# A two-layer kernel with a mixture of experts: queue places by products, logits read in PSUM, turned inputs written by ScalarE, four result buffers

## The chip, the cores and the metric

One core of a Trainium2 chip runs the whole program. The time is the device time of that core in microseconds (us), from the first to the last instruction of one execution; less is better. The kernel before takes 1167.64 us, the median of three runs (1167.55 to 1169.25).

## The reference, cut to what matters

Two layers run one after the other on `x`, 4 batches of 512 tokens of 256 values, all in float32. Layer 0 is the one that the change touches:

```python
h = _layernorm(x) * (1 + ca) + sa               # ca, sa, ga ...: per batch, from silu(c) @ wmod
q, k, v = split(h @ W + b, 3)
x = x + ga * (q / |q| * sum_t(k / |k| * v))     # norms and sum over the 512 tokens
h = _layernorm(x) * (1 + cb) + sb
...
logits = h @ gate_w.T                           # 2048 tokens x 32 experts, in 8 groups of 4
# the 3 groups with the largest maximum are kept, the other logits become 0; softmax;
# the 6 largest are chosen, weights times 16
pos = cumsum(one_hot(chosen)) - 1               # place in the expert's queue, token after token
valid = pos < 48                                # an expert takes 48 tokens, the rest get zero
act = silu(xb @ w_gate) * (xb @ w_up)           # per expert, inner size 176
yb = act @ w_down
out = sum_k(topk_w * yb[slot]) + shared_experts(h)
x = x + gb * out
```

Layer 1 is causal attention with 16 heads of 128 for each batch and a gated feed-forward net whose weights are interpolated from control points.

## The kernel before, in words

Tokens lie on the 128 partitions: a batch is four tiles of 128 tokens (`NTT` = 4). A product needs the values on the partitions instead, so every norm ends in transpositions on TensorE (PE) and an eviction that also applies the modulation. The program runs in three stages.

**The front** (0 to 150.3 us) goes through the batches. `attention_input` normalises a batch and turns it; `linear_attention`, in two halves, projects v, k and q and forms the attention; `attention_output` turns the result back and adds it to x; `moe_input` is the second norm, turned into `hTs[b]`; `choose` makes logits and picks six experts for each token; `table_rows` writes the tokens to a table in DRAM, its arithmetic on GpSimd (POOL, L534 and L535); `place` finds each token's place in its expert's queue. Each engine works off its instructions in order. In the front that order is made by the framework's scheduler from the program, which puts the products of the shared experts (`shared`, L704), which need only `hTs`, between the others on PE. After the last batch a small product (`pid`, L686) gives the list of tokens for every expert.

What the change touches there:

- `ln_transposed` (L217): for each half k of the 256 values, four transpositions (L226) into a PSUM tile of tag "tr", and one eviction: k = 0 by ScalarE (ACT, L228), k = 1 by VectorE (DVE, L232). The tag has two banks, shared in the front with the attention's output on its way back (`add_transposed`, L237) and with the logits.
- `choose` (L542): eight products put the logits into a bank of tag "tr" (L547); DVE copies them to SBUF (L555), reduces them to group maxima (L559), finds the three best (`max`, L562, `match_replace`, L566), makes the mask `keep` (L568) and multiplies (L572); softmax is a maximum (L580), a subtraction, ACT's exp (L584), a sum and a division. L592 to L595 turn probabilities into keys (a probability below `TINY` gets a low key), L598 to L604 choose six, `selb` being the 0/1 matrix in bf16. L608 and L610 then form `pre`: for each tile of 128 tokens, the number of choices that lie in earlier tiles and earlier batches, kept for each partition and each expert; `carry` hands it from batch to batch.
- `place` (L615): two products make the place. `tri` (L619), 1 where the row of the token is below, counts the choices in the same tile; `ones` (L622) sums `pre` over the partitions. L626 then adds -200 where the token is chosen, L628 adds 200 and cuts at 255, so that tokens not chosen end at a large number: `posb`. Its one-hot form against 48 places (L650) goes through products with the token numbers (L654) into `ixs` (L661). The tiles `pos`, `pix` and `pid` share one bank, tag "lgix".

**The experts** (150.3 to 237.3 us) are 16 pairs of experts, 64 rows each. The order on PE is written out by hand here: gather (`xg`), transposition, `gate_up` (L805), `act_turned`, `down` (L828), with the shared experts' second product between them. Weights have 8 slots, loaded by SP's queue. `down` leaves a pair's result in PSUM (`y`, one bank), and ACT writes it, times the token's weight, to an SBUF tile `ysb` (L842). For pairs 0 to 11 that tile has tag "ysb", of two buffers, and two DMAs read it: POOL's scatter to `planes` (L858), for the tokens of batch 0, and SP's write to `ytab` (L873), from which the other batches gather later. Pairs 12 to 15 have tag "ysd", four buffers, and come to batch 0 through a product instead of a scatter. Then SP reads `planes` back (L912) and DVE sums.

**Layer 1** (from 248 to 1166 us) begins with the norm of batch 0. It calls `ln_transposed` too.

Of the kernel before, what the change touches and what calls it, by code (L numbers as in the profile page):

```python
# [10 lines left out]
F32 = mybir.dt.float32  # L11
BF16 = mybir.dt.bfloat16
I32 = mybir.dt.int32
AF = mybir.ActivationFunctionType
ALU = mybir.AluOpType
AX = mybir.AxisListType

P = 128
B, T, D = 4, 512, 256
NT = B * T  # L20
NTT = T // P
# [4 lines left out]
E, G, TOPG, TOPK, CAP, INT = 32, 8, 3, 6, 48, 176  # L26
# [7 lines left out]
NDIR = 4  # L34
NEARLY = 6
TINY = float(np.finfo(np.float32).tiny)
# [44 lines left out]
def kernel(ctx: ExitStack, tc: tile.TileContext, a: dict, out: bass.AP):  # L81
    nc = tc.nc
# [19 lines left out]
    SA, CA, GA, SB, CB, GB = range(6)  # L102
# [111 lines left out]
                )  # L214
        return xn

    def ln_transposed(pool, psum, tag, layer, b, shift, scale, hT, name, bufs=None, after=None, scalar_after=None):  # L217

        xn = normalized(pool, b, name, bufs, after, scalar_after)
        for k in range(2):  # L220
            if isinstance(tag, tuple):
                pt = psum.tile([P, T], F32, tag=tag[k], name=f"lt_{name}{b}{k}", bufs=1)
            else:
                pt = psum.tile([P, T], F32, tag=tag, name=f"lt_{name}{b}{k}")
            for i in range(NTT):
                nc.tensor.transpose(pt[:, i * P : (i + 1) * P], xn[:, i, k * P : (k + 1) * P], ident)  # L226
            if k == 0:
                nc.scalar.activation(  # L228
                    hT[:, k, :], pt, AF.Identity, bias=mv(layer, shift, k, b), scale=mv(layer, scale, k, b)
                )  # L230
            else:
                last = nc.vector.tensor_scalar(  # L232
                    hT[:, k, :], pt, mv(layer, scale, k, b), mv(layer, shift, k, b), ALU.mult, ALU.add
                )
        return xn, last
# [66 lines left out]
    with ExitStack() as l0:  # L302
        moe = l0.enter_context(tc.tile_pool(name="moe", bufs=1))
        front = ExitStack()
        fc = front.enter_context(tc.tile_pool(name="frontc", bufs=1, side="right"))
        rp = front.enter_context(tc.tile_pool(name="route", bufs=2, side="right"))
# [15 lines left out]
        )  # L322
        didx = moe.tile([P, NPAIR], I32, tag="didx", name="didx")

        carry = fc.tile([P, E], BF16, tag="carry", name="carry")
        nc.gpsimd.memset(carry, 0.0)

        zeroed, last, hTa = [], {}, {}
        with tc.tile_pool(name="mod0", bufs=1) as mp:
# [13 lines left out]
            with tc.manual_schedule(engines={mybir.EngineType.PE}):  # L343
# [19 lines left out]
                out=wsd[:, 0:2, :], in_=a["ws_down"][0 : 2 * P].rearrange("(c p) n -> p c n", p=P)  # L363
            )
            nc.sync.dma_start(out=wsd[0 : SHC[2], 2, :], in_=a["ws_down"][2 * P : 2 * INT])
            for v, src in enumerate((S0[64:68, D:], S0[96:100, 0:D], g4)):
# [3 lines left out]
                out=rows.rearrange("p v b d -> p (v b d)"),  # L370
                in_=flat[:, 0 : 2 * B * D].to_broadcast([P, 2 * B * D]),
            )
            nc.sync.dma_start(
                out=gbr.rearrange("p b d -> p (b d)"),
                in_=flat[:, 2 * B * D :].to_broadcast([P, B * D]),
# [8 lines left out]
            for i in range(NTT):  # L384
                fill = nc.sync.dma_start(
                    out=planes[i * P * TOPK : (i + 1) * P * TOPK, :].rearrange("(p r) d -> p (r d)", p=P),
                    in_=zero,
                )
# [3 lines left out]
        def constants():  # L392

            tri = fc.tile([P, P], BF16, tag="tri", name="tri")
            nc.gpsimd.memset(tri, 1.0)
            nc.gpsimd.affine_select(
                out=tri, in_=tri, compare_op=ALU.is_gt, fill=0.0, base=0,
                pattern=[[1, P]], channel_multiplier=-1,
            )
            ones = fc.tile([P, P], BF16, tag="ones", name="ones")  # L400
            nc.gpsimd.memset(ones, 1.0)
            iota_c = fc.tile([P, CAP, E], BF16, tag="iota_c", name="iota_c")
            nc.gpsimd.iota(
                iota_c, [[1, CAP], [0, E]], base=0, channel_multiplier=0,
                allow_small_or_imprecise_dtypes=True,
            )

            tok = fc.tile([P, NI, 32], BF16, tag="tok", name="tok")
            nc.gpsimd.memset(tok, 0.0)
            nc.gpsimd.iota(  # L410
                tok[:, :, 0], [[0, NI]], base=0, channel_multiplier=1, allow_small_or_imprecise_dtypes=True
            )
            nc.gpsimd.iota(
                tok[:, :, 1], [[P, NI]], base=-NT, channel_multiplier=0, allow_small_or_imprecise_dtypes=True
            )

            two = fc.tile([P, 4], F32, tag="two", name="two")
            nc.gpsimd.memset(two, 0.0)
            for q in range(4):
                nc.gpsimd.memset(two[32 * q : 32 * q + 2, q : q + 1], 1.0)  # L420

            six = fc.tile([P, NTT, 1], F32, tag="six", name="six")
            nc.gpsimd.iota(
                six, [[P * TOPK, NTT], [0, 1]], base=0, channel_multiplier=TOPK,
                allow_small_or_imprecise_dtypes=True,
            )

            first = moe.tile([P, 1, E], F32, tag="first", name="first")
            nc.gpsimd.iota(
                first, [[0, 1], [EPAD, E]], base=1, channel_multiplier=0,  # L430
                allow_small_or_imprecise_dtypes=True,
            )

            gss, dps = [], []
            for u in range(2):
                gs = fc.tile([P, NTT, 16], F32, tag=f"gs{u}", name=f"gs{u}")
                nc.gpsimd.memset(gs[:, :, G:], 3.0e38)
                gss.append(gs)
                dp = fc.tile([P, NTT, E + 8], F32, tag=f"dp{u}", name=f"dp{u}")
                nc.gpsimd.memset(dp[:, :, E:], 1.0)  # L440
                dps.append(dp)

            ixs = fc.tile([P, EPAD, 8], F32, tag="ixs", name="ixs")
            nc.gpsimd.memset(ixs, 0.0)

            return tri, ones, iota_c, tok, two, six, first, gss, dps, ixs
# [28 lines left out]
        hTs, posbs = {}, {}  # L475

        def attention_input(b, sp, ps):
            hT = hTa[b] = sp.tile([P, 2, T], F32, tag="hTa", name=f"hT_a0{b}")
            _, last[b] = ln_transposed(sp, ps, "tr", 0, b, SA, CA, hT, "a0", 3, last[b - 1])

        oTs0, xns = {}, {}

# [41 lines left out]
        def moe_input(b, sp, ps):  # L524

            hTs[b] = new_hT(hp, b, "m0")
            xn, _ = ln_transposed(sp, ps, "tr", 0, b, SB, CB, hTs[b], "m0", 3)
            xns[b] = xn

        def table_rows(b):  # L530
# [9 lines left out]
        chosen = {}  # L540

        def choose(b, ps):  # L542

            lgv = ps.tile([P, NTT, E], F32, tag="tr", name=f"plg{b}")
            for i in range(NTT):
                for k in range(2):
# [4 lines left out]
                        start=(k == 0),  # L551
                        stop=(k == 1),
                    )
            lg = rp.tile([P, NTT, E], F32, tag="lg", name=f"lg{b}")
            nc.vector.tensor_copy(lg, lgv)  # L555
            lg4 = lg.rearrange("p i (g j) -> p i g j", g=G)

            gs, dp = gss[b % 2], dps[b % 2]
# [24 lines left out]
            wt = wr[:, :, 0, :]  # L583
# [5 lines left out]


            sel = rp.tile([P, NTT, E], F32, tag="sel", name=f"sel{b}")
            nc.vector.tensor_single_scalar(sel, wt, TINY, ALU.is_ge)  # L592
            nc.vector.tensor_tensor(sc, sc, sel, ALU.mult)
            nc.vector.tensor_scalar(sel, sel, -1.0, 100.0, ALU.add, ALU.mult)
            nc.vector.tensor_tensor(dp[:, :, 0:E], sc, sel, ALU.add)  # L595
            m8 = rp.tile([P, NTT, 8], F32, tag="m8", name=f"em8{b}")
            for i in range(NTT):
                nc.vector.max(m8[:, i, :], dp[:, i, 0:E])  # L598
# [4 lines left out]
            selb = rp.tile([P, NTT, E], BF16, tag="selb", name=f"selb{b}")  # L603
            nc.vector.tensor_single_scalar(selb, dr[:, :, 0:E], 1.5, ALU.is_gt)  # L604
            nc.vector.scalar_tensor_tensor(wt, wt, SCALE, selb, ALU.mult, ALU.mult)

            pre = rp.tile([P, NTT, E], BF16, tag="pre", name=f"pre{b}")
            nc.vector.tensor_copy(pre[:, 0, :], carry)  # L608
            for i in range(NTT):
                nc.vector.tensor_tensor(  # L610
                    pre[:, i + 1, :] if i + 1 < NTT else carry, pre[:, i, :], selb[:, i, :], ALU.add
                )
            chosen[b] = sel, selb, pre, wr

        def place(b):  # L615

            sel, selb, pre, wr = chosen[b]
            pos = psa.tile([P, NTT, E], F32, tag="lgix", name=f"pos{b}", bufs=1)
            nc.tensor.matmul(  # L619
                pos.rearrange("p i e -> p (i e)"), lhsT=tri, rhs=selb.rearrange("p i e -> p (i e)"), start=True, stop=False  # L620
            )
            nc.tensor.matmul(  # L622
                pos.rearrange("p i e -> p (i e)"), lhsT=ones, rhs=pre.rearrange("p i e -> p (i e)"), start=False, stop=True
            )

            nc.vector.scalar_tensor_tensor(sel, selb, -200.0, pos, ALU.mult, ALU.add)  # L626
            posb = posbs[b] = moe.tile([P, NTT, E], BF16, tag=f"posb{b}", name=f"posb{b}")
            nc.vector.tensor_scalar(posb, sel, 200.0, 255.0, ALU.add, ALU.min)  # L628
            if b:

                nc.gpsimd.memset(wr[:, :, 1, :], float(1 << 20))
# [147 lines left out]
        with tc.tile_pool(name="eps", bufs=2, space=PSUM) as ps:  # L779
# [43 lines left out]
            def down(q):  # L823
                wd = loaded[q][1]
                py = ps.tile([P, D], F32, tag="y", name=f"y{q}", bufs=1)
                for c in range(2):
# [7 lines left out]
                        )  # L834
                direct = q >= NPAIR - NDIR
                ysb = xp.tile(
                    [P, D], F32, tag=("ysb", "ysd")[direct], name=f"ysb{q}", bufs=(2, NDIR)[direct]
                )
                for j in range(2):
                    rows_ = slice(EPAD * j, EPAD * j + EPAD)  # L840
# [966 lines left out]
```

## Time and profile before

| What | Value |
|---|---|
| median of three runs | 1167.64 us (1167.55 to 1169.25) |
| the profiled execution's own time | 1168.07 us |
| its span, from first to last recorded work | 1166.0 us |
| mean granted PE clock | 0.993 |
| PE busy (share of the span) | 1118.2 us (96%), 5220 products |
| PE weight loads | 821.9 us (70%) |
| DVE | 859.4 us (74%), 2601 instructions |
| ACT | 536.2 us (46%), 1373 |
| POOL | 619.4 us (53%), 944 |
| DMA | 86.09 MB, mean 74 GB/s |

How to read it: the profile is one execution, recorded by the chip. "Busy" adds up the durations of an engine's instructions; a share of 96% over the whole span says little of a single stage, so the tables of the prediction are cut by stage. In a group of instructions, "out<-in" gives the program's names of the tiles, "L610" the line, "x12" how often, and then stand the busy time, the mean duration in ns and the idle time of the engine just before, with what ended it. "PEclk" or "granted clock" is the share of full speed that TensorE was given. The span is cut in 40 slices on the page, of 29 us each; these are the rows of PE and DVE in tenths of busy time, 9 being 90% or more:

```profile
PE   6888998989999999999999999999999999999998
DVE  5688624567878887788877887988877777567765
```

The first five or six slices are the front, the next three the experts, and the rest layer 1.

### The profile page before, as it was taken

The page shows a single profiled execution, that of the slowest core. Times are in us where ns is not written, and L with a number is a line of the kernel's source. Part 1 is how long each engine was busy: PE and PEld are TensorE (multiplying, and loading weights), DVE is VectorE, ACT ScalarE, POOL GpSimd, SP SyncE. Part 2 cuts the span into 40 slices and gives each one's busy share as a digit, 9 for nine tenths or more (in the row PEclk, how much of TensorE's full clock was granted, in tenths as well). Part 3 has the DMA queues.
Part 4 walks back from the last instruction along what each step waited for, and adds up shares of the span by engine and source line. Part 5 has one row for each costly group of instructions (what it writes and reads, how often), then busy time and mean ns, then how long its engine had stood idle before and what let it go on. Part 6 is the DMA issues. An engine that isn't in the chain of part 4 may idle for free.

```text
span 1166.0 us, 16905 instructions
## 1 busy us (share of the span) xinstructions
PE 1118.2 (96%) x5220; PEld 821.9 (70%) x5220; DVE 859.4 (74%) x2601; ACT 536.2 (46%) x1373; POOL 619.4 (53%) x944
## 2 busy tenths in 40 slices
PE   6888998989999999999999999999999999999998
PEld 2434354557777787777777777777777777888887
DVE  5688624567878887788877887988877777567765
ACT  3543223335555555554555465555555455333321
POOL 3354124338874857864665975444635655344331
PEclk9998999999999999999999999999999999999999
DMA  8910389734411322420321431012010000000001
GB/s 266 292 61 23 101 238 281 237 106 87 85 47 51 73 69 37 86 73 19 86 37 46 95 64 60 28 37 65 23 46 19 22 16 1 1 1 19 19 1 37
DMA packets 80485, 86.09 MB, mean 74 GB/s; under 512 B 12158, under 2 KB 64748, under 8 KB 80268
## 3 DMA queue, kind: packets, MB, share of 16 engines
q1 hardware_dynamic: 67868, 70.19, 19.2%
q0 software_dynamic: 11712, 13.25, 7.1%
q10 hardware_dynamic: 816, 1.58, 0.4%
q8 instruction: 42, 0.69, 0.3%
q14 instruction: 47, 0.39, 0.1%
HBM read 73.84 MB, written 11.55 MB: 73 GB/s over the span
## 4 chain that ended last, share of the span: by engine, by line
PE 64%; DVE 8%; POOL 3%; ACT 2%; issue 1%; DMA 1%; SPq 0%; ACTq 0%; DVEq 0%; POOLq 0%
PE s L1299 10%; PE o L1340 10%; PE po L1035 7%; PE P0p L1035 6%; PE fP L1035 6%; PE pt L1331 5%; PE P1p L1035 4%; PE P2p L1035 4%; PE acc L1035 3%; PE P0v L1035 3%; PE P2v L1035 2%; PE P1v L1035 2%; DMA w_q<-in_w_q 1%; POOL ysum L281 1%; DVE spw L1130 1%
## 5 line engine op out<-in xcount | busy, mean ns | idle before, releaser
L1314 ACT ACTIVATE p<-s,nm 128x512 f32<-128x512 f32 (+3 forms) x256 | 135.2, 528 | 116.0 <-DVE nm L1311 113.9
L1299 PE MATMUL s<-qk,qk 128*128 128x512 f32 (+3 forms) x512 | 170.1, 434 | 1.4 <-DVE qk L1207 1.3
L1340 PE MATMUL o<-pT,v 128*128 128x512 f32 (+3 forms) x512 | 148.6, 433 | 0.1
L1340 PEld LDWEIGHTS o<-pT,v 128*128 128x128 f32 x512 | 96.8, 190 | 55.0 <-issue 30.6
L1333 ACT COPY pT<-pt 128x512 f32<-128x512 f32 (+1 forms) x192 | 98.3, 512 | 67.8 <-PE pt L1331 66.7
L1311 DVE TENSOR_REDUCE nm<-s 128x1 f32<-128x512 f32 (+3 forms) x256 | 124.0, 485 | 4.0
L281 POOL DMA_INDIRECT ysum<-ytab,code x72 | 113.5, 1576 | 20.4 <-issue 15.2
L1316 DVE TENSOR_SCALAR p<-p,den 128x512 f32<-128x512 f32 (+3 forms) x256 | 116.2, 454 | 3.4
L1331 PEld LDWEIGHTS pt<-ident,p 128*128 128x128 f32 x640 | 81.6, 141 | 34.4 <-issue 10.5
L1331 PE MATMUL pt<-ident,p 128*128 128x128 f32 x640 | 101.7, 273 | 0.4 <-DVE p L1316 0.4
L1309 DVE TENSOR_TENSOR s<-s,mask 128x128 f32<-128x128 f32 x256 | 73.4, 287 | 32.6 <-PE s L1299 32.6
L1174 POOL TENSOR_TENSOR w_p<-w_q,w_k 128x128 f32<-128x128 f32 x63 | 38.6, 613 | 85.2 <-ACT t1p L1213 52.3
L1299 PEld LDWEIGHTS s<-qk,qk 128*128 128x128 f32 x512 | 77.5, 191 | 5.8 <-issue 1.4
L1035 PE MATMUL P0p<-hT_a,w_q 128*128 128x256 f32 x252 | 75.0, 379 | 0.0
L1182 POOL TENSOR_TENSOR w_p<-w_k 128x128 f32<-128x128 f32 x63 | 29.7, 472 | 81.4 <-PE P2p L1035 81.4
L1035 PEld LDWEIGHTS P0p<-hT_a,w_q 128*128 128x128 f32 x252 | 47.5, 190 | 33.1 <-issue 29.9
L1315 DVE RECIPROCAL den<-den 128x1 f32<-128x1 f32 x256 | 40.4, 158 | 38.3 <-ACT p L1314 33.6
L1035 PE MATMUL P1p<-fT,w_p 128*128 128x256 f32 x252 | 64.9, 380 | 2.4 <-POOL w_p L1176 1.3
L1351 ACT ACTIVATE oH<-o,bia 128x512 f32<-128x512 f32 x64 | 43.9, 687 | 42.9 <-PE o L1340 41.7
L1207 DVE SCALAR_TENSOR_TENSOR qk<-P0p,bia,u3p 128x256 f32<-128x256 f32 x63 | 30.4, 482 | 37.4 <-ACT qk L1228 36.4
L1043 POOL TENSOR_TENSOR fI<-it 128x256 f32<-128x256 f32 x30 | 21.8, 726 | 67.1 <-DVE it L1632 67.1
L1035 PEld LDWEIGHTS P1p<-fT,w_p 128*128 128x128 f32 x252 | 47.6, 190 | 9.9 <-issue 1.8
(338 smaller groups left out, 2677.7 us busy)
## 6 DMA issues: line engine op xcount, KB each, us to landing
wg<-in_w_gate_up SPq DMA_DIRECT2D x16, 704.0 KB
w_q<-in_w_q SPq DMA_DIRECT2D x64, 128.0 KB
w_k<-in_w_k SPq DMA_DIRECT2D x64, 128.0 KB
w_v<-in_w_v SPq DMA_DIRECT2D x16, 512.0 KB
wd<-in_w_down SPq DMA_DIRECT2D x16, 352.0 KB
basis<-in_basis SPq DMA_DIRECT2D x8, 640.0 KB
planes<-zero SPq DMA_DIRECT2D x4, 768.0 KB
yr<-planes SPq DMA_DIRECT2D x4, 768.0 KB
```

The source lines that it names most:

```text
L281: ga = nc.gpsimd.indirect_dma_start(out=ysum[b][:, i, :], out_offset=None, in_=ytab[:, :], in_offset=bass.IndirectOffsetOnAxis(ap=code[:, ...
L1035: nc.tensor.matmul(out, lhsT=lhsT, rhs=rhs, start=start, stop=stop, skip_group_check=shared)
L1299: nc.tensor.matmul(s[:, at[i] : c], lhsT=qk[n, 0][:, i * P : (i + 1) * P], rhs=qk[n, 1][:, : (i + 1) * P], start=True, stop=True,)
L1309: nc.vector.tensor_tensor(s[:, e - P : e], s[:, e - P : e], mask, ALU.add)
L1311: nc.vector.tensor_reduce(nm, s[:, e - w : e], AX.X, ALU.max, negate=True)
L1314: nc.scalar.activation(p, s[:, e - w : e], AF.Exp, bias=nm, accum_out=den)
L1315: nc.vector.reciprocal(den, den)
L1316: nc.vector.tensor_scalar_mul(p, p, den)
L1331: nc.tensor.transpose(pt[:, c : c + P], probs[n, i][:, j * P : (j + 1) * P], ident)
L1333: nc.scalar.copy(pT, pt[:, :w])
L1340: nc.tensor.matmul(o[:, j * P :], lhsT=vs[n // 4][:, j, hc : hc + HD], rhs=pTs[n, j], start=(j == 0), stop=(j == NTT - 1),)
L1351: nc.scalar.activation(oT, o, AF.Identity, bias=bia[:, 2, h : h + 1])
```

## The change

1. `ln_transposed` gets an argument `both`. Where it is set, in `attention_input` and `moe_input` of layer 0 (three and four calls), ACT does both evictions. Layer 1 is as before.
2. The logits are not copied: L559 and L572 read them in PSUM, so their bank is held until the product with `keep`.
3. L592 to L595, four DVE instructions, become three.
4. `tri` gets -200 on its diagonal, through one more GpSimd mask instruction. The -200 of L626 thereby comes out of the product, and L626 goes; `posb` is made from PSUM directly.
5. The running sums in `pre` go. For each batch but the last, DVE adds up its four `selb` tiles and the carry before (3, 4 and 4 additions). The place is made by products alone: `tri` with `selb`, `ones` with the carry (repeated for all four tiles), and `ones` with each earlier tile (repeated for the later ones): 4 products for batch 0 and 5 for each other batch, 19 in place of 8.
6. Tag "ysb" has four buffers instead of two.

The core of the diff:

```diff
-            if k == 0:
-                nc.scalar.activation(
+            if k == 0 or both:
+                last = nc.scalar.activation(
...
+            nc.gpsimd.affine_select(
+                out=tri, in_=tri, compare_op=ALU.not_equal, fill=-200.0, base=0,
+                pattern=[[1, P]], channel_multiplier=-1,
+            )
...
-            _, last[b] = ln_transposed(sp, ps, "tr", 0, b, SA, CA, hT, "a0", 3, last[b - 1])
+            _, last[b] = ln_transposed(sp, ps, "tr", 0, b, SA, CA, hT, "a0", 3, last[b - 1], both=True)
...
-            xn, _ = ln_transposed(sp, ps, "tr", 0, b, SB, CB, hTs[b], "m0", 3)
+            xn, _ = ln_transposed(sp, ps, "tr", 0, b, SB, CB, hTs[b], "m0", 3, both=True)
...
-            lg = rp.tile([P, NTT, E], F32, tag="lg", name=f"lg{b}")
-            nc.vector.tensor_copy(lg, lgv)
+            lg = lgv
...
-            nc.vector.tensor_single_scalar(sel, wt, TINY, ALU.is_ge)
-            nc.vector.tensor_tensor(sc, sc, sel, ALU.mult)
-            nc.vector.tensor_scalar(sel, sel, -1.0, 100.0, ALU.add, ALU.mult)
-            nc.vector.tensor_tensor(dp[:, :, 0:E], sc, sel, ALU.add)
+            nc.vector.scalar_tensor_tensor(sc, wt, TINY, sc, ALU.is_ge, ALU.mult)
+            nc.vector.tensor_scalar(sel, wt, TINY, -1.0, ALU.is_ge, ALU.add)
+            nc.vector.scalar_tensor_tensor(dp[:, :, 0:E], sel, 100.0, sc, ALU.mult, ALU.add)
...
-            pre = rp.tile([P, NTT, E], BF16, tag="pre", name=f"pre{b}")
-            nc.vector.tensor_copy(pre[:, 0, :], carry)
-            for i in range(NTT):
-                nc.vector.tensor_tensor(
-                    pre[:, i + 1, :] if i + 1 < NTT else carry, pre[:, i, :], selb[:, i, :], ALU.add
-                )
-            chosen[b] = sel, selb, pre, wr
+            chosen[b] = selb, wr
+            if b + 1 < B:
+
+                c = carry[b + 1] = rp.tile([P, 1, E], BF16, tag="carry", name=f"carry{b}")
+                parts = [selb[:, i, :] for i in range(NTT)] + ([carry[b][:, 0, :]] if b else [])
+                nc.vector.tensor_tensor(c[:, 0, :], parts[0], parts[1], ALU.add)
+                for x in parts[2:]:
+                    nc.vector.tensor_tensor(c[:, 0, :], c[:, 0, :], x, ALU.add)
...
+            nc.tensor.matmul(pos, lhsT=tri, rhs=selb, start=True, stop=False)
+            if b:
+                nc.tensor.matmul(
+                    pos, lhsT=ones, rhs=carry[b].to_broadcast([P, NTT, E]), start=False, stop=False
                 )
...
+            for i in range(1, NTT):
+                nc.tensor.matmul(
+                    pos[:, i:, :],
+                    lhsT=ones,
+                    rhs=selb[:, i - 1 : i, :].to_broadcast([P, NTT - i, E]),
+                    start=False,
+                    stop=(i == NTT - 1),
+                )
...
-            nc.vector.scalar_tensor_tensor(sel, selb, -200.0, pos, ALU.mult, ALU.add)
             posb = posbs[b] = moe.tile([P, NTT, E], BF16, tag=f"posb{b}", name=f"posb{b}")
-            nc.vector.tensor_scalar(posb, sel, 200.0, 255.0, ALU.add, ALU.min)
+            nc.vector.tensor_scalar(posb, pos, 200.0, 255.0, ALU.add, ALU.min)
...
-                    [P, D], F32, tag=("ysb", "ysd")[direct], name=f"ysb{q}", bufs=(2, NDIR)[direct]
+                    [P, D], F32, tag=("ysb", "ysd")[direct], name=f"ysb{q}", bufs=4
```

More of the change, by code (lines that the diff above doesn't have):

```diff
@@ L215, in normalized, with ln_transposed @@
         return xn
-    def ln_transposed(pool, psum, tag, layer, b, shift, scale, hT, name, bufs=None, after=None, scalar_after=None):
+    def ln_transposed(pool, psum, tag, layer, b, shift, scale, hT, name, bufs=None, after=None, scalar_after=None, both=False):
         xn = normalized(pool, b, name, bufs, after, scalar_after)
@@ L323 @@
         didx = moe.tile([P, NPAIR], I32, tag="didx", name="didx")
-        carry = fc.tile([P, E], BF16, tag="carry", name="carry")
-        nc.gpsimd.memset(carry, 0.0)
+        carry = {}
         zeroed, last, hTa = [], {}, {}
@@ L605, in choose @@
             nc.vector.scalar_tensor_tensor(wt, wt, SCALE, selb, ALU.mult, ALU.mult)
-            pre = rp.tile([P, NTT, E], BF16, tag="pre", name=f"pre{b}")
-            nc.vector.tensor_copy(pre[:, 0, :], carry)
-            for i in range(NTT):
-                nc.vector.tensor_tensor(
-                    pre[:, i + 1, :] if i + 1 < NTT else carry, pre[:, i, :], selb[:, i, :], ALU.add
-                )
-            chosen[b] = sel, selb, pre, wr
[L615 to L620, printed above, removed]
-            )
[L622 to L626, printed above, removed]
+            chosen[b] = selb, wr
@@ new lines, in choose, with place @@
+            if b + 1 < B:
[4 more added lines that the diff above has]
+                    nc.vector.tensor_tensor(c[:, 0, :], c[:, 0, :], x, ALU.add)
+        def place(b):
+            selb, wr = chosen[b]
+            pos = psa.tile([P, NTT, E], F32, tag="lgix", name=f"pos{b}", bufs=1)
+            nc.tensor.matmul(pos, lhsT=tri, rhs=selb, start=True, stop=False)
+            if b:
+                nc.tensor.matmul(
+                    pos, lhsT=ones, rhs=carry[b].to_broadcast([P, NTT, E]), start=False, stop=False
+                )
+            for i in range(1, NTT):
[6 more added lines that the diff above has]
+                )
```

## The prediction

> **What bounds the kernel now.** First, the busy time of each engine by stage: stretch and length in us, then PE, weight load, DVE, ACT and POOL in busy us (instructions), granted PE clock, DMA share, GB/s.
>
> ```profile
> 0.00:60.00 60.00, 46.36 (x158) 21.63 (x159) 36.66 (x131) 25.75 (x50) 23.06 (x54) 0.97 0.85 278
> 60.00:130.00 70.00, 58.73 (x231) 27.25 (x231) 61.50 (x248) 26.36 (x45) 28.30 (x44) 0.95 0.19 61
> 130.00:150.30 20.30, 20.30 (x75) 8.30 (x74) 8.23 (x14) 2.98 (x5) 7.90 (x8) 1.00 0.24 63
> 150.30:237.30 87.00, 82.51 (x461) 46.78 (x459) 41.45 (x145) 29.20 (x70) 27.35 (x30) 0.98 0.85 262
> 237.30:248.00 10.70, 7.30 (x21) 4.06 (x22) 5.61 (x13) 3.18 (x6) 5.55 (x9) 0.84 0.22 78
> 248.00:1166.00 918.00, 903.05 (x4281) 713.89 (x4279) 705.93 (x2053) 448.73 (x1199) 527.20 (x799) 1.00 0.19 44
> ```
>
> From 248 us on (layer 1) PE is busy 98% of the time, and the built programs have the same order there on every engine; what is won or lost earlier is passed on whole. All edits lie in the front (to 150.3) and the experts (150.3 to 237.3). In the front's middle, 60 to 130 us, DVE is the fullest engine (61.5 of 70 us); PE idles 70 - 58.7 = 11.3 us and runs at clock 0.95 (3.5 us lost). From 130 us PE has no gap: it works off the shared expert's products, which wait for little. So the front ends when PE's fixed work plus its gaps are over; the gaps can be won.
>
> Second, who PE waits for from 10 to 150 us (total us, times, longest), then the groups of instructions up to 150 us that the edits touch (busy us, mean ns | idle before).
>
> ```profile
> PE lt_a L226 <- DVE xn_a L212: 6.4, 5, 2.1
> PE pix L654 <- DVE oh L650: 3.0, 5, 0.9
> PE su L704 <- DVE sT L713: 2.7, 2, 1.6
> PE lt_m L226 <- DVE xn_m L212: 2.5, 4, 1.0
> ```
>
> ```profile
> L610 DVE TENSOR_TENSOR pre<-pre,selb 128x32 bf16<-128x32 bf16 x12 | 4.5, 377 | 0.1
> L232 DVE TENSOR_SCALAR hT_m<-lt_m,mod 128x512 f32<-128x512 f32 x4 | 3.2, 803 | 0.0
> ...
> L626 DVE SCALAR_TENSOR_TENSOR sel<-selb,pos 128x128 f32<-128x128 bf16 x4 | 1.1, 281 | 0.1
> ```
>
> ```profile
> L228 ACT ACTIVATE hT_m<-lt_m,mod 128x512 f32<-128x512 f32 x4 | 3.1, 769 | 0.8 <-PE lt_m L226 0.8
> ```
>
> PE's waits name DVE; ACT is busy for 26 of the 70 us. Third, the experts: who waits (115 to 290 us), and PE in order of time (start, us, what, idle before it).
>
> ```profile
> PE y L828 <- ACT ysb L842: 4.2, 4, 1.9
> ...
> ACT ysb L842 <- DMA ytab<-ysb: 8.2, 3, 3.7
> ...
> ACT ysb L842 <- DMA planes<-ysb,didx: 4.6, 2, 3.3
> ```
>
> ```profile
> 177.55 1.08 PE L828 MATMUL y<-wd,actT 88*64 88x256 f32 x8 [1.02 <-ACT ysb L842]
> ...
> 189.87 1.75 PE L828 MATMUL y<-wd,actT 88*64 88x256 f32 x8 [1.92 <-ACT ysb L842]
> 191.40 2.43 PE L805 MATMUL gu<-wg,xT 128*64 128x352 f32 x8
> ...
> 240.50 0.41 PE L226 MATMUL lt_a<-ident,xn_a 128*128 128x128 f32 x2 [3.24 <-DMA basis<-in_basis]
> ```
>
> All four PE waits from pair 2 to the last scattered pair end at a ysb write on ACT, and ACT waits there for DMAs that still read the buffer of two pairs before: about 10 us from issue (the table write of pair 0 is issued at 166.19; ACT goes on at 176.55), while a pair takes 3 to 4 us. The last wait (240.50; the DMA named there feeds no transposition) ends a chain: last scatter issued at 214.7, planes read back from 217.3, DVE sums from 225.3 to 234.8, norm, transposition. It starts from pair 11, so it moves with it.
>
> **The change, part by part.** Sums are against the profiled execution (1168.07 us, span 1166.0); the median of the runs is 0.4 lower.
>
> *DVE in the front.* Removed: seven turned inputs, 7 x 0.80 = 5.6 us; four logit copies (L555, 0.286 each) 1.1; four rounds of L592 to L595 (0.341 + 0.392 + 0.216 + 0.409 = 1.36 each) become three instructions priced like L593, L592 and L595 (1.14): 0.9; L608 and L610 (4 x 0.168 + 12 x 0.377 + 4 x 0.284 = 6.3) become 11 additions (3, 4, 4, none): at 0.377 they cost 4.1, so 2.2 (4.4 if at the 0.17 of the undisturbed ones); L626, 4 x 0.281 = 1.1. Together 10.9 us busy; rows start about 0.08 before the one ahead ends, and 28 rows go, so 8.7 us of DVE time: 2.8 before 60 us, 5.9 after. What is late next: DVE's waits for POOL's power (about 1.1 us each), for ACT and for PE do not shrink, so I take half of the 5.9 (3.0 us), and 1.0 of the lt_a waits before 60 us, where DVE is only 61% full. Bounds: nothing, and 5.9 + 2.8.
>
> *Turned inputs on ScalarE.* The second eviction of each pair runs after the first instead of beside it: 0.69 us later (0.77 less an overlap of 0.08), seven times, 4.8 us, if nothing covers it. The new PE order puts 2.1 us of shared products and position products between the last transposition and the first logit product that needs it (third batch), and projections in the attention layer norms; I charge 0.5. Queued behind on ACT: squares, exp and silu writes. The page "ScalarE: Activation LUTs" (section Rules for kernel authors) speaks against this: multiply and add belong on VectorE, up to about three times faster, in bf16. The rows here are 0.803 on DVE and 0.769 on ACT for the same f32 PSUM tile. Were DVE three times faster, the seven would free 7 x 0.26 = 1.8 us, not 5.6, and the part would lose; by the rows it wins. I take the rows.
>
> *Places by products.* 19 position products replace 8. The L622 row is 0.22 us, but the next product starts 0.06 later: 11 x 0.06 = 0.7 us of PE, at most 11 x 0.22 = 2.4. In return the product no longer waits for the running sum (the pos wait was 1.9 us). The extra GpSimd mask (0.4, as the first one) lies at 14 us, with POOL then idle for 1.67 us before 18.22: nothing; its successors are constants used after 55 us. Without that cover, 0.4.
>
> *Logits in PSUM.* The bank is released at the product with keep instead of the copy: 3.6, 6.1, 9.9 and 2.4 us after the copy (55.20 to 58.80, 68.90 to 75.01, 96.00 to 105.92, 116.78 to 119.15). Two banks serve this tag, and the second half of the next batch's attention transposition needs one. The new order puts projections or one-hot products between, so I charge 0.5; at worst 2 us for each of three batches, and not below nothing, since nothing else gets a bank sooner. A reduction reading PSUM: L559's 0.277 stays, as L626 read PSUM at 0.281.
>
> *Clock in the front.* 3.5 us are lost at half clock around 94 to 104 us, after gaps. Fewer gaps may save it or shift it; from +3.5 to -3.5, I take a gain of 1.0.
>
> Front: 3.0 + 1.0 + 1.0 - 0.5 - 0.7 - 0.5, some 3.3; with 0.7 for the position wait (a third of 1.9, the rest is in the 3.0) 4.0 us.
>
> *Four result buffers.* ysb q now waits for pair q - 4: 12 to 16 us against a DMA time of about 10. The four waits (1.02, 1.92, 0.66, 0.62) go: 4.2 us. After the second, y takes 1.75 for 1.08 and gu 2.43 for 1.40 at a granted clock of 0.83 over 190 to 200: 1.7 us more. The page "TensorE: Matmul & The Clock Gate" (section HAM oscillation) asks only for no PE gap above about 3.4 us; by it a 1.92 gap costs itself, and this part gives 4.2. The row shows a half-clock spell behind it, so 5.9. Late next are the weights: 0.85 of the DMA engines is busy, and PE asks sooner. I take 5.0; bounds 0 and 5.9.
>
> Layer 1: nothing, plus or minus 1.
>
> Sum: 4.0 + 5.0 = 9.0; 1167.64 - 9.0 = **1158.6 us**.
>
> **Rivals.** B, *the front does not move*: ScalarE's later writes and POOL's power chain take back what DVE gives; only the buffers count, 1167.64 - 5.0 = 1162.6. For it: 4.8 us of serial eviction; against: every long PE wait names DVE. C, *the buffers do not do what they say*: the wait passes from ysb to weights or scatters; front only, 1163.6. For it: DMA at 0.85 and up to 324 GB/s; against: PE never waits for weights now, and between 210 and 220 us DMA is half idle. D, *slower, by ScalarE*: the second batches' turned inputs stand in ACT's queue behind a table load (1.28) and a silu write (0.60), which the new order puts between ACT's share of the norm and the third batch's eviction. All seven late evictions uncovered cost 4.8, this 1.9, two more half-clock spells 3.4, DVE's relief then shows nowhere: 10.1 lost, 5.0 won, 1172.7. It decides from where ACT is over 2.1 us late after the last transposition, the filler that PE has.
>
> **How the numbers follow.** The likeliest, A (both gains), has 0.55: its range is 1153.5 (front 8, experts 6) to 1163.5. B 0.18, C 0.09, D 0.18. The range 1153 to 1168 holds A, B, C and the mild third of D. A measurement tells 0.2% (2.3 us) from no change: faster is under 1165.3 (A 0.54, B 0.15, C 0.08: 0.77), slower over 1169.9 (D 0.15), the rest 0.08.
>
> **What would show it.** Right: the last shared product ends at 144 to 149 us instead of 150.3; DVE busy in the front down by about 11; no PE y wait on ysb; no spell near 190; the first layer 1 transposition at 230 to 233. Wrong: PE waits for hT on ScalarE (D); PE gaps before gu or y that name DMA (C); layer 1 not 918 us long.

## The result, and the profile after

The changed kernel took 1162.72 us against 1170.79 us for the kernel before (medians of eight runs each). The ratio is 0.9928, with a 95% interval of 0.9908 to 0.9948: 8.4 us less, or 6.1 to 10.7. A second set of runs gave 0.9908 (0.9887 to 0.9929). The forecast was 9.0 us less, 0.9923 as a ratio. The sum was right. Its two terms were less so: in the experiments the front gave 7.2 us (4.9 to 9.7) for its 4.0, and the buffers about 3 us, with as much either way, for their 5.0.

The kernel before is less steady than its first three runs said: its runs went from 1166.7 to 1176.8 us, and the execution profiled for the prediction (1168.07) was one of its quicker ones. The changed kernel's profiled execution (1165.69, span 1164.0) was one of its slower ones, among runs from 1158.1 to 1166.5. The two profiles differ by 2.0 us of span, so they explain mechanisms, not the 8.4 us.

First the stages of the changed kernel, cut at the same times as before (columns as there: PE, weight load, DVE, ACT, POOL, clock, DMA share, GB/s):

```profile
0.00:60.00 60.00, 48.56 (x163) 23.14 (x164) 35.35 (x138) 30.97 (x58) 23.13 (x54) 1.00 0.84 274
60.00:130.00 70.00, 58.19 (x249) 26.95 (x248) 57.50 (x222) 25.87 (x44) 28.68 (x44) 0.95 0.20 66
150.30:237.30 87.00, 80.63 (x452) 45.16 (x450) 41.51 (x148) 29.36 (x70) 28.44 (x30) 0.96 0.85 262
248.00:1166.00 918.00, 901.15 (x4272) 712.02 (x4270) 705.13 (x2049) 448.20 (x1196) 528.10 (x799) 1.00 0.19 44
```

DVE is down from 61.50 to 57.50 us between 60 and 130 us, but PE still does only 58.19 of 70 us there, at the same clock of 0.95. PE is ahead through the first 60 us (48.56 for 46.36). Then who PE waits for from 10 to 150 us (total us, times, longest):

```profile
PE lt_m L226 <- DVE xn_m L212: 4.9, 4, 2.6
PE lt_a L226 <- DVE xn_a L212: 3.9, 3, 1.7
PE pix L663 <- DVE oh L659: 3.5, 2, 2.0
PE sg L713 <- ACT sT L721: 2.5, 2, 1.8
...
PE at_a L244 <- DVE sc L575: 0.6, 1, 0.6
...
PE pos L622 <- DVE selb L606: 0.2, 1, 0.2
```

Before, these three stood there too:

```profile
PE pos L622 <- DVE pre L610: 1.9, 2, 1.6
PE sg L704 <- ACT sT L712: 1.1, 2, 0.7
PE lt_m L226 <- DVE ssum L587: 1.0, 1, 1.0
```

The waits for normalised rows before the attention fell from 6.4 to 3.9 us, the wait of the place product from 1.9 to 0.2. The second norm's rose (2.5 and 1.0 before, 4.9 now), and so did that of the shared products for ACT (1.1, now 2.5). No line names an eviction of turned inputs on ACT. One line is new: the attention's way back waits 0.6 us for the product with `keep` (L575), which now holds its PSUM bank. The groups:

```profile
L228 ACT ACTIVATE hT_m<-lt_m,mod 128x512 f32<-128x512 f32 x8 | 5.8, 773 | 0.0
L615 DVE TENSOR_TENSOR carry<-carry,selb 128x32 bf16<-128x32 bf16 x6 | 2.3, 392 | 0.1
L562 DVE TENSOR_REDUCE gs<-plg 128x32 f32<-128x128 f32 x4 | 1.1, 282 | 0.0
```

An eviction on ACT takes 0.77 us, an addition for the carry as long as before (0.39, before 0.38), and a reduction that reads PSUM as long as one from SBUF (0.282 against 0.277).

Now the experts. All four waits of `y` for `ysb` are gone from PE. In their place stands one longer one (PE in order of time: start, us, what, idle before):

```profile
200.82 1.08 PE L837 MATMUL y<-wd,actT 88*64 88x256 f32 x8
201.84 0.46 PE L167 MATMUL pmt<-ident,mrows 64*128 64x64 f32 x4
206.37 2.61 PE L814 MATMUL gu<-wg,xT 128*64 128x352 f32 x8 [4.07 <-DVE xT L807]
208.91 0.66 PE L828 MATMUL act_t<-ident,act 128*88 128x128 f32 x2
```

DVE's copy of `xT` is only the last link. Follow it back through ACT, DVE and SP's queue in the same stretch (same columns): DVE stood behind the product of `act` (L823), and that waited for ACT.

```profile
199.04 0.58 ACT L159 COPY mrows<-pm 64x512 f32<-64x512 f32 x1 [0.91 <-PE pm L152]
204.85 0.42 ACT L770 ACTIVATE w_q<-w_q 128x256 f32<-128x256 f32 x1 [5.22 <-DMA w_q<-in_w_q]
205.29 0.32 ACT L822 ACTIVATE act<-gu 128x176 f32<-128x176 f32 x1
```

```profile
205.64 0.34 DVE L823 TENSOR_TENSOR act<-act,gu 128x176 f32<-128x176 f32 x1 [4.53 <-ACT act L822]
205.90 0.42 DVE L807 COPY xT<-xt 128x256 f32<-128x256 f32 x1
```

```profile
193.82 0.38 SPq L754 DMA_DIRECT2D w_q<-in_w_q  x1
```

L770 scales layer 1's first query weights. Nothing in the experts needs it, but it stands in ACT's queue in front of a pair's silu write, and its load, issued at 193.82, has not landed. ACT waits 5.22 us, DVE 4.53, PE 4.07, and the four groups after the gap run at half clock (2.61 us for `gu` where 1.40 is usual). The kernel before has the same instruction at the same place, and in its profile ACT does not wait there:

```profile
207.09 0.95 ACT L842 ACTIVATE ysb<-y,xg 64x256 f32<-64x256 f32 x2
208.06 0.42 ACT L761 ACTIVATE w_q<-w_q 128x256 f32<-128x256 f32 x1
```

Its load was issued at 197.20 there, and ACT reached the scaling 10.9 us later, held up by ysb waits until the load had landed. In the changed kernel ACT got there 5.8 us after the issue (199.04 + 0.58 - 193.82).

### The profile page after: what moved, and what is told of

The parts are those of the page before. It is cut to its first block, busy times and chain, and to the rows that moved or that the text cites. A ratio compares the mean times of both kernels' runs of the same rounds, so it can differ in the third digit from the quotient of the medians.

```text
span 1164.0 us, 16910 instructions
## 1 busy us (share of the span) xinstructions
PE 1118.4 (96%) x5231; PEld 822.6 (71%) x5231; DVE 850.9 (73%) x2573; ACT 541.5 (47%) x1380; POOL 621.0 (53%) x944
## 4 chain that ended last, share of the span: by engine, by line
PE 72%; DVE 8%; POOL 4%; ACT 3%; issue 2%; DMA 2%; SPq 0%; ACTq 0%; POOLq 0%; DVEq 0%
PE s L1308 10%; PE o L1349 10%; PE po L1044 7%; PE P0p L1044 6%; PE fP L1044 6%; PE pt L1340 5%; PE P1p L1044 4%; PE P2p L1044 4%; PE acc L1044 3%; PE P0v L1044 3%; PE P2v L1044 2%; PE P1v L1044 2%; POOL ysum L281 1%; PE gu L814 1%; PE sg L713 1%
```

## The experiments

Theory M says that the buffers' gain is real, but that a part of it runs into the wait for `w_q`. Rival R1: this wait is an accident of the one profiled execution. Rival R2: the DMA engines bound the experts, whatever PE waits for. Ratios are to the kernel before, with 95% intervals; 0.1% is 1.17 us. From each kernel one execution was profiled.

**The buffers alone.** `buffers_only` is the kernel before with

```diff
-                    [P, D], F32, tag=("ysb", "ysd")[direct], name=f"ysb{q}", bufs=(2, NDIR)[direct]
+                    [P, D], F32, tag=("ysb", "ysd")[direct], name=f"ysb{q}", bufs=4
```

> The kernel before with four ysb buffers and nothing else. Theory M (the four y waits on ysb go, but in many executions the scaling of layer 1's first w_q on ScalarE, which stands ahead of a pair's silu write, then waits for its DMA and PE pays): PE shows no y wait on ysb, ACT waits for w_q up to 5 us between 195 and 210 us, and the time is 0 to 6 us under before, the last y product 0 to 6 us earlier relative to the end of the front. Rival R1 (that wait is an accident of one execution): 4 to 6 us under before, ACT's wait for w_q about 1 us. Rival R2 (DMA alone is the bound of this stage): 0 +- 1 us, and the waits pass to the weights or to the gathers.

Measured: 1.0029 (1.0015 to 1.0044), 3.4 us slower. No case had that. The order of instructions tells why the edit is not alone: with other buffers the scheduler chose another order, in the front, on ACT (the `w_q` scaling stands ahead of the write of pair 9, no longer behind it) and on SP's queue. There two loads of spline windows (L1540, for layer 1) and weight loads stand ahead of the first `ytab` write (SP's queue; the second column is the time that the issue took):

```profile
161.27 0.37 SPq L1540 DMA_DIRECT2D win<-in_windows  x1
163.12 2.91 SPq L458 DMA_DIRECT2D wg<-in_w_gate_up  x1
166.44 4.64 SPq L1540 DMA_DIRECT2D win<-in_windows  x1
171.19 2.86 SPq L462 DMA_DIRECT2D wd<-in_w_down  x1
174.15 0.35 SPq L873 DMA_DIRECT2D ytab<-ysb  x1
```

The result of pair 0 was ready at 165.36 (164.41 + 0.95); its write was issued at 174.15, before the change at 166.19. ACT's waits for `ytab` reads of old results rose to 15.8 us, and the wait for `w_q` was 7.68.

**The window loads out of the way.** `buffers_win_late` is `buffers_only` with, in effect,

```diff
-                    nc.sync.dma_start(out=win[:, j, :, :], ...)
+                    wait_for(nc.sync.dma_start(out=win[:, j, :, :], ...), [wrote[0]])
```

where `wrote[0]` is the latest ysb write.

> The kernel before with four ysb buffers, as in buffers_only, and the three loads of spline windows made to wait for the last ysb write, so that they can't stand ahead of the experts' weights on SP's queue. Theory W (buffers alone lost because the scheduler put two of these loads ahead of weights and of the first ytab write, which was issued 8 us later): the first ytab write is issued at 165 to 167 us, ACT's waits for ytab fall from 15.8 to under 6 us, and the time is 2 to 5 us under before. Rival R2 (more results in flight only load the DMA engines more): the waits for ytab stay above 10 us and the time is not under before.

Measured: 1.0078 (1.0049 to 1.0106), slower still. So the window loads, as theory W has them, are not the cause of the time: the first `ytab` write is now issued at 162.69, right behind the data (161.72 + 0.95). But the writes of pairs 2 to 7 still leave 3 to 4 us after their data, where in the changed kernel those up to pair 6 leave with the data. A weight load that stands earlier on SP's queue here is the likely reason; no run tests it. ACT's waits for `ytab` are 10.2 us here, so what R2 named (over 10, and no gain) is what came. ACT in the profile:

```profile
195.89 0.95 ACT L842 ACTIVATE ysb<-y,xg 64x256 f32<-64x256 f32 x2 [3.91 <-DMA ytab<-ysb]
206.05 0.42 ACT L761 ACTIVATE w_q<-w_q 128x256 f32<-128x256 f32 x1 [9.21 <-DMA w_q<-in_w_q]
206.49 0.32 ACT L813 ACTIVATE act<-gu 128x176 f32<-128x176 f32 x1
```

The scaling stands a whole pair earlier here, before the silu write and the write of pair 9. ACT reached it at 196.84, 1.0 us after its load was issued (195.80), and waited 9.2; PE waited 7.7:

```profile
207.57 2.62 PE L805 MATMUL gu<-wg,xT 128*64 128x352 f32 x8 [7.74 <-DVE xT L798]
```

**The scaling out of the way.** `scale_late` is the changed kernel with

```diff
-        for n in range(3):
-            scale_q(n)
+        with tc.issue_after(wrote[0].ins):
+            [scale_q(n) for n in range(3)]
```

which puts the three scalings after the last ysb write on ACT and moves nothing else on any engine.

> The changed kernel with the three scalings of w_q placed after the last ysb write on ScalarE's queue; nothing else moves on any engine. Theory M: no PE wait for xT near 201 us, the experts 4 to 6 us shorter than in the profiled execution of the changed kernel, the time 2 to 6 us under the changed kernel's. Rival R1: the same as the changed kernel within 1 us. Rival R2: PE's wait comes back at a later pair, with weights or gathers named, and the time is the changed kernel's.

Measured: 0.9893 (0.9869 to 0.9916), 12.5 us under before and the lowest ratio of all; in the same set the changed kernel has 0.9908, so 1.6 us by medians (1160.12 and 1161.67), which their spread does not quite tell from nothing. In the profile the wait is gone and the experts take 84.2 us instead of 90.5. `scale_win_late` moves the window loads too:

> The changed kernel with the scalings of w_q after the last ysb write, as in scale_late, and the window loads late as well. Theory M: the scalings were the one wait left, so it gains 2 to 4 us over the changed kernel, as scale_late did, and the window loads add under 1 us. If SP's queue held ytab writes back there too: 1 to 2 us more than scale_late.

Measured: 0.9897 (0.9875 to 0.9920). The window loads add nothing that can be measured in this order.

**The changed kernel once more.**

> The changed kernel once more, for a second profiled execution. Theory M: ACT's wait for w_q near 200 us is there again, between 2 and 6 us. Rival R1: it is under 2 us, and the experts' stage is 4 to 5 us shorter than in the first profile. Time 0.993 +- 0.002 of before.

Measured: 0.9908, and in the profile the wait is there again:

```profile
204.47 0.42 ACT L770 ACTIVATE w_q<-w_q 128x256 f32<-128x256 f32 x1 [3.08 <-DMA w_q<-in_w_q]
```

It was 3.08 us here and 5.22 in the first profile (and 3.34 in `no_both` below). R1 falls: the wait is regular, its length is not.

**The same on the old front.** `buffers_scale_late` is `buffers_win_late` with the scalings late, `before_scale_late` the kernel before with the scalings late; each differs from its parent on ACT alone.

> The front of before, four ysb buffers, window loads late, and the w_q scalings after the last ysb write. It differs from buffers_win_late on ScalarE's queue alone. Theory M (the scaling's wait, moved one pair earlier by the scheduler, cost buffers_win_late its 9 us): 8 to 12 us under buffers_win_late, 0.992 to 0.997 of before, no PE wait for xT near 205 us. Rival R2: under 3 us of it come back, the waits pass to weights or gathers, and it stays at or over before.

> The kernel before with the w_q scalings after the last ysb write, two buffers. Theory M (with two buffers PE comes late enough that w_q has landed): the same as before within 1.5 us. If the scaling's wait costs before too: 2 to 5 us under before.

Measured: 0.9955 (0.9940 to 0.9970) and 0.9984 (0.9969 to 0.9998). With four buffers the late scaling is worth 1.2%, 12 us by medians (1178.06 to 1165.83), with two buffers 0.2%, just clear of nothing, so it is not quite free there either. That is theory M: the scaling, one pair too early, is what made `buffers_win_late` a loss. For `buffers_only` itself, with the window loads early, it is not shown alone. R2 falls in the form it was stated: once this wait is gone, the time comes down without fewer bytes. But four buffers do not end the waits in this order of SP's queue (`buffers_scale_late`, 115 to 290 us):

```profile
ACT ysb L842 <- DMA ytab<-ysb: 17.2, 6, 4.6
...
PE y L828 <- ACT ysb L842: 5.2, 3, 2.8
```

**The front alone.** `front_only` is the changed kernel with two ysb buffers, `front_scale_late` the same with the scalings late.

> The changed kernel with two ysb buffers as before: the front's edits alone. Theory M: the last shared product at 147 to 149 us, and the time 2 to 4 us under before; the ysb waits are back (3 to 5 us). If instead the front carries most of the change's gain: 6 to 9 us under before.

> scale_late with two ysb buffers again: with the w_q scaling out of the way, this and scale_late differ in the buffers alone. Theory M (the buffers' gain is real, and the wait for w_q hid most of it in the changed kernel): 4 to 6 us over scale_late, so 0.993 to 0.995 of before, PE's waits for ysb 3 to 5 us. Rival R2 (transfers bound this stage anyway): within 1.5 us of scale_late.

Measured: 0.9938 (0.9917 to 0.9958) and 0.9941 (0.9922 to 0.9960). The waits for `ysb` are back on PE; in `front_scale_late` they are

```profile
PE y L837 <- ACT ysb L851: 3.7, 4, 2.3
```

So the front's edits are worth 0.62%, 7.2 us, and the buffers what is left: 3.1 us in the changed kernel (1164.75 to 1161.67, same set, about 3.4 us either way, so hardly told from nothing), and 5.4 us with the scaling late (0.9941 to 0.9893, about 3.6 us either way). On the old front they gave 3.4 us (0.9984 to 0.9955, about 2.4 either way), with the late writes above. With two buffers a few instructions of ACT, POOL and SP's queue also change places in the experts, so this is the buffers together with that order.

**Parts of the front.** `no_both` is the changed kernel without `both=True` in its two calls. `old_places_late` is `scale_win_late` with `pre`, the two products and L626 as before.

> The changed kernel with the second eviction of layer 0's turned inputs on VectorE again: what part 1 of the change brings. If the relief of VectorE carries the front (5.6 of 10.9 us of the busy time won): 1.5 to 3 us over the changed kernel, pid 1.5 to 3 us later than at 133. If the serial eviction on ScalarE takes it back: within 0.7 us of the changed kernel, or under it.

> scale_win_late with the places made as before (running sums in pre by VectorE, two products, the -200 by VectorE): parts 4 and 5 of the change undone. By the prediction these parts took 3.3 us of VectorE's busy time and the 1.9 us wait for pre: pid 1 to 3 us later and the time 1 to 2.5 us over scale_win_late. Rival (the 11 extra products on PE cost as much as they save): within 0.7 us of it.

Measured: 0.9956 (0.9940 to 0.9971), so the ScalarE evictions are worth 3 to 6 us (the changed kernel had 0.9928 and 0.9908; each difference about 3 us either way); and 0.9931 (0.9905 to 0.9956) against 0.9897, about 4 us with an interval that reaches down to nothing. Both kernels also have another order in the front, and `old_places_late` on SP's queue as well, so neither is its edit alone. In the profile of `no_both` the list of tokens (`pid`) comes at 136.1 us (133.4 and 135.1 in the changed kernel), but the front ends no later (147.1). In that of `old_places_late` `pid` comes at 140.9 us (132.6 in `scale_win_late`), far later than the forecast, the front is 2.5 us longer and the experts 4.8: there `ytab` writes leave 3 to 5 us late again, and PE waits 2.9 us for `ysb`. In the front PE waits in `place`:

```profile
PE pos L620 <- DVE pre L608: 3.2, 2, 1.7
PE pos L617 <- DVE selb L602: 2.3, 3, 1.1
```

These 5.5 us are 0.3 us (`selb` alone) in `scale_win_late`. And `no_both` shows two waits for the eviction on DVE:

```profile
PE plg L551 <- DVE hT_m L232: 1.3, 2, 1.0
```

**The kernel before once more.**

> The kernel before once more, unchanged, for a second profiled execution: the first one was 3 us under the median of all runs since. Theory E (the executions differ in the experts, where ysb waits and transfers meet): front and layer 1 agree within 1.5 us with the first profile, and from the last shared product to layer 1's first transposition it takes 92 to 96 us instead of 90.6. Rival F (the front differs): the last shared product ends 2 to 4 us later than 149.9.

Measured: 1.0007 (0.9991 to 1.0024), span 1170.9 us in the profile. Theory E holds: the front ended 0.8 us later, layer 1 took 0.7 us more, the experts 3.4 us more. The stages of all these profiles, in us (the front up to the start of the last shared product, the experts from there to layer 1's first transposition, then the rest):

| Kernel | front | experts | rest | span | ratio of the runs |
|---|---|---|---|---|---|
| before | 149.9 | 90.6 | 925.5 | 1166.0 | 1 |
| before, again | 150.7 | 94.0 | 926.2 | 1170.9 | 1.0007 |
| before_scale_late | 150.6 | 89.4 | 927.2 | 1167.2 | 0.9984 |
| buffers_only | 147.8 | 98.4 | 928.8 | 1175.0 | 1.0029 |
| buffers_win_late | 145.2 | 98.9 | 928.6 | 1172.7 | 1.0078 |
| buffers_scale_late | 148.0 | 89.8 | 926.4 | 1164.2 | 0.9955 |
| front_only | 147.3 | 88.6 | 926.6 | 1162.5 | 0.9938 |
| front_scale_late | 148.2 | 89.5 | 925.8 | 1163.5 | 0.9941 |
| changed | 147.9 | 90.5 | 925.6 | 1164.0 | 0.9928 |
| changed, again | 149.6 | 87.1 | 927.8 | 1164.5 | 0.9908 |
| scale_late | 147.2 | 84.2 | 926.7 | 1158.1 | 0.9893 |
| scale_win_late | 147.1 | 83.4 | 928.1 | 1158.6 | 0.9897 |
| no_both | 147.1 | 88.9 | 926.4 | 1162.4 | 0.9956 |
| old_places_late | 149.6 | 88.2 | 926.3 | 1164.1 | 0.9931 |

## Why the prediction was right, and where it was not

*The sum.* Predicted 9.0 us, measured 8.4 and, in the second set, 10.8. That it came out so near is in part luck: two terms missed in opposite directions.

*Layer 1 passes everything on.* Right: 925.5 to 928.8 us in all 14 profiles. The forecast allowed one us either way; the profiles lie up to 3.3 us apart.

*DVE in the front.* The busy time was about right: predicted 10.9 us less, measured 9.1 (106.39 us up to 149.9 before, 97.32 up to 147.9 after). The 11 additions took 3.8 us (predicted 4.1). The new three instructions took 1.04 us a round (predicted 1.14).

*What it is worth, "front 4.0".* This term was mis-sized: too small. By the runs the front gave 7.2 us (4.9 to 9.7), and 5.0 and 6.8 in the two other pairs (`before_scale_late` to `front_scale_late`, `buffers_scale_late` to `scale_win_late`), each about 3 us either way. In the profiles its end moved from between 149.9 and 150.7 to between 147.1 and 149.6, about 2.5 us on average. The list of tokens (`pid`) moved further, from 138.0 to 133.4: the shared products behind it are PE work that has to be done all the same. The other 2.5 to 4.7 us appear, if anywhere, in the experts with two buffers (88.6 and 89.5 us against 90.6, 94.0 and 89.4). One profile of each kernel, where repeats differ by 3.4 us, can't settle where they lie, and that stays open.

*Turned inputs on ScalarE, "I charge 0.5".* Right, and rival D with it falls. No PE wait names ACT's evictions; the weight loads before the logits waited 0.5 and 0.3 us for them. The measured durations (0.77 on ACT, 0.80 on DVE) held; the rule of the Trainium skill, "ScalarE: Activation LUTs" (Rules for kernel authors), that was weighed against them gives its factor for bf16. Taken for these f32 rows from PSUM it would have had this part lose, and undoing the part cost 3 to 6 us, order included.

*Places by products.* The costs were right: the products start 0.06 us apart (111.31, 111.37, 111.42), and the wait of 1.9 us is 0.2. What the part is worth in time stays open (see `old_places_late`).

*Logits in PSUM, "I charge 0.5".* Right: 0.6 us, the wait of the attention's way back for L575.

*Clock in the front, "a gain of 1.0".* Not seen: 0.95 between 60 and 130 us in both, 0.92 and 0.89 from 60 to 124 in other profiles of this front.

*Four result buffers, "Late next are the weights ... I take 5.0".* This step failed. The four waits and the half-clock spell went as worked out. (The fourth, 0.62 us, had not been a buffer's: before, ACT wrote that `ysb` at 211.34 right behind a silu write, without a DMA wait; in the changed order it is gone too. And the "about 10 us from issue" is the first write's, 10.4; the later waits ended 6 to 9 us after the issue.) In the changed kernel the buffers of pairs 0 to 5 were written again 12.5 to 15.6 us after the issue, as forecast. But what was late next was not an expert's weights. It was layer 1's `w_q`, through one scaling in ACT's queue that the prediction didn't count: in the first profile 4.07 us of PE wait and 2.2 us of half clock behind (1.21 for `gu`, 0.20, 0.23 and 0.58 for the next three), 6.3 in all for the 5.9 us removed. That fits a stage of 90.5 us after 90.6, as far as single profiles tell. The sign that was named for a right forecast, layer 1's first transposition at 230 to 233 us, came at 238.4 and 236.7; with the scaling late it came at 231.4. By the runs the buffers were worth about 3 us; with the scaling moved, 5.4. So 5.0 fits the buffers without this wait, and rival C is the mechanism that took a share, at a place it did not name; how large a share the runs of the changed kernel hardly resolve.

*The rule on gaps.* The Trainium skill, "TensorE: Matmul & The Clock Gate" (HAM oscillation), asks only for gaps under about 3.4 us. The 4.07 us gap fits that, though half clock set in 2.0 us into it (at 204.30). Gaps of 1.92 us in `changed, again` (`gu` 2.61 us), 1.92 in the kernel before and 2.05 in `front_only` (`y` 1.94 us) were followed by half clock too, while 1.98 in `buffers_only`, 1.96 in `buffers_win_late` and even 2.81 in `buffers_scale_late` were not (`y` 1.08 us, and full speed after). So the gap's length alone doesn't decide it. Its place tells most of it, by the granted clock in these profiles: the complete half-clock spells last 3.41 us or a multiple, and within a profile they begin on one grid of 3.41 us. The gap of the kernel before (187.95 to 189.87) lies in one step of its grid, that of `buffers_scale_late` (189.56 to 192.37) is split, 1.78 and 1.03 us (columns as above, PE busy first, clock third from the end):

```profile
186.73:190.14 3.41, 1.49 (x12) 0.71 (x9) 0.57 (x2) 1.24 (x3) 0.70 (x2) 1.00 0.82 259
190.14:193.55 3.41, 3.41 (x16) 1.45 (x12) 2.60 (x13) 0.02 (x1) 2.13 (x2) 0.50 0.85 292
```

```profile
187.92:191.33 3.41, 1.63 (x12) 0.74 (x8) 1.80 (x11) 0.00 (x0) 1.19 (x1) 1.00 0.97 274
191.33:194.75 3.42, 2.38 (x12) 0.84 (x12) 0.87 (x4) 1.26 (x3) 1.86 (x2) 1.00 0.81 257
```

From 145 to 240 us, in all 14 profiles, each of the 17 steps at full clock in which PE idled 1.92 us or more was followed by half clock, and none of those with up to 1.18 us was; of the six between, three were.

## What to carry to other kernels

When a wait is taken away, list every instruction that stands in the freed engine's queue behind it, up to the end of the stage, and ask for each when its data lands: here one early instruction of the next layer, nearly free as long as the engine came 10 us late, took back some 2 of 5 us (barely clear of noise), and on the old front more than all. A change of a buffer count can reorder queues that it doesn't touch, so a part tried alone is only that part if the orders are compared. And where repeats of one kernel differ by 5 us of span (1166.0 and 1170.9), 2 us between two profiles say nothing of the sum; repeated runs do.

## What the runs showed of the hardware

An issue on SP's queue is not always short: a load of spline windows took 0.37 us to issue at one place and 4.64 at another, and a weight load 2.9, where 0.3 to 0.4 is usual; what stands behind them in the queue, here writes that free a buffer, waits as long. From issue to use, the first `w_q` load (128 KB) took 11.0, 11.2, 10.3, 9.1 and 10.6 us in the five profiles in which ACT waited for it (changed, changed again, buffers_win_late, buffers_only, no_both). And a PE gap of 1.92 us could cost a half-clock spell of 3.41 us where one of 2.81 us cost none: as far as these profiles show, what counted was PE's idle time within one step of a 3.41 us grid.
